# Gate convolution with its rows packed as source, row and channel, in four 32-column tiles

## The chip, the cores and the metric

The kernel runs on one core of one Trainium2 chip. The metric is the device time of one execution in microseconds; three runs of the kernel before gave a median of 13,861.98 us (13,850.41 to 13,873.61). Engines are named as in the profile: PE is TensorE (PEld its weight loads), DVE VectorE, ACT ScalarE, POOL GpSimd, and SPq the queue of SyncE, which here issues nearly all DMAs.

## The reference

A batch of 32 images with 8 channels of 256 x 256 goes through two residual layers, each with a group normalisation ahead of it (4 groups of 2 channels).

```python
# layer 0, on x normalised
grid = drive = x
for _ in range(15):
    mapped = 3.9 * grid * (1.0 - grid)
    local = conv3x3(mapped, K_local, groups=8)         # depthwise
    physics = 0.7 * mapped + 0.3 * local
    grid = 0.85 * physics + 0.15 * drive
cml_out = clip(grid, 0.0001, 0.9999)
h = relu(conv3x3(x, Wp, bp))                           # 8 -> 128
nca_out = sigmoid(conv1x1(h, Wu, bu))                  # 128 -> 8
gin = concatenate([x, cml_out, nca_out], axis=1)       # 24 channels
g = sigmoid(conv1x1(relu(conv3x3(gin, Wg1, bg1)), Wg2, bg2))
layer0 = g * cml_out + (1.0 - g) * nca_out
# layer 1: both operands quantised to +-127, conv3x3 8 -> 8, scaled back, plus bias
```

The gate convolution is the 3 x 3 convolution with Wg1 over the 24 channels of gin, to 8 channels.

## The kernel before

Images are worked in eight groups of four (GB = 4). Five kinds of work, each written as a generator that yields a weight after each piece:

- `prep`/`normalise` (L301): loads x, normalises it, and writes to DRAM scratch a permuted copy for the lattice (xq_s, made by ACT at L370: the pixels of a row ordered by their column modulo four) and a padded high/low pair for NCA (xp_s).
- `lattice` (L396): the 15 steps on grid, a channel of the group's four images at a time, all of it resident in SBUF. A step is three tiles of 6 matmuls (L511), with DVE operations from PSUM (L519, L524), a small POOL product at the edges (L528), and at the end of tiles 1 and 2 an exchange of halo rows by two DMAs each (L474, L475) that the next step needs. After each tile up to three DMAs of a backlog (unit loads d_a, result stores to cm_s; L464) are issued by `background`.
- `nca` (L581): the 8 to 128 convolution (L591, two row tiles of 48 rows), relu on ACT (h, L601), the 128 to 8 product in four 32-column tiles (L608), sigmoid (L626), store to nc_s.
- `gate` (L745): described below.
- the second layer, in a section of its own from L936, after all groups.

TensorE's order is written out by hand: `together` (L870) runs a lattice step and then as many pieces of the filler as keep both in proportion, and `both` (L884) mixes NCA, the gate of the group before, and prep by the totals T_NCA = 520, T_GATE = 340, T_PREP = 34 and T_LATTICE = 709 (L916). The other engines' order is made by the scheduler of the framework from the program's order and its own estimates[...]. The last group's gates run alone at the end (L930).

The gate before: an image is 19 tiles of 14 output rows, with 16 rows x 8 channels on the 128 partitions (two halo rows). A piece p takes two tiles, and there are ten per image, the last with one tile. `stage` (L691) loads nc_s (nb), cm_s (cq) and the raw x (xb, one DMA per tile). `arrange` (L719), called two yields later, unpermutes cq to natural order on POOL (L723), normalises xb on DVE (L729), and makes d = cml - nca and f = x + nca on POOL (L735, L736). The convolution (L795) is three sources x three column shifts x two 64-column halves, with 128 x 128 banded weights gw, spread over three yields of 3.5 and 2.6. Then relu on ACT (L812), and one piece later `finish` (L752): the 1 x 1 product (L758), sigmoid (L760), y = gate * d + f on DVE (L762, L763), statistics (L771 to L773). The store of y to y_s is issued one piece later still (L802).

## Time and profile before

| | |
|---|---|
| median of three runs | 13,861.98 us |
| the profiled execution: its time and span | 13,862.1 us |
| PE busy | 13,134.4 us, 95% |
| DVE, ACT, POOL busy | 59%, 29%, 18% |
| L511 lattice matmuls, on the m_a and the m_b side (these two run at once) | 5,842.6 and 5,809.7 us |
| L591 NCA convolution, high and low weights (overlapping) | 2,685.1 and 2,569.9 us |
| L608 NCA product | 1,155.1 us |
| L795 gate convolution, by source cmb, xnb, nb | 861.4, 847.8 and 847.2 us |
| L758 gate product | 319.8 us |
| DMA moved, share of the 16 engines | 1,496.77 MB, 46% |
| mean granted TensorE clock | 0.975 |

An fp32 matmul appears in the trace as two passes, so a count in the profile is twice the number in the program. A group's busy time counts a stretch once when several of its instructions overlap in it, and matmuls overlap with their neighbours, so prices of matmuls are better read from the start of one to the start of the next. DMA issues do not count as busy time of SP; they are read from SP's queue in the timeline.

### The profile page before, as it was taken

To read this page: it belongs to the slowest core of one execution; us is meant where nothing else is said; L and a number is where in the kernel's file an instruction comes from. 1 tells how busy PE (TensorE), PEld (TensorE's weight loads), DVE (VectorE), ACT (ScalarE), POOL (GpSimd) and SP (SyncE) were. 2 spreads that over 40 slices of the span, in tenths; PEclk is the share of its full clock that TensorE was granted. 3 is DMA by queue.
4 is the path that set the end of the run, shared out by engine and by line. 5 is a ranking of instruction groups with operands and counts; after the bars stand their busy time and mean duration, and the time that the engine had idled before them with its cause. 6 is when DMAs were issued, how large, how long until landed. Compare 5 with 4: busy or idle time off the path is not lost.

```text
span 13862.1 us, 229831 instructions
## 1 busy us (share of the span) xinstructions
PE 13134.4 (95%) x81840; PEld 6403.4 (46%) x81840; DVE 8176.8 (59%) x16402; ACT 4028.2 (29%) x6274; POOL 2454.7 (18%) x4278
## 2 busy tenths in 40 slices
PE   4899999999999999999999999999999999999964
PEld 2445544444444444444444444444444444444322
DVE  5555565566655565555655565555655555555577
ACT  2233223232322223322323223222223222222123
POOL 1001111121111211111111111112111111111310
PEclk8999999999999999999999999999999999999986
DMA  6444444444444444444444444444444433333368
GB/s 152 96 97 99 96 104 112 101 98 101 111 99 103 109 93 108 108 104 93 107 106 101 102 104 103 102 106 108 94 108 110 100 91 84 89 79 89 90 202 257
DMA packets 2287210, 1496.77 MB, mean 108 GB/s; under 512 B 1096576, under 2 KB 2257152, under 8 KB 2285952
## 3 DMA queue, kind: packets, MB, share of 16 engines
q1 hardware_dynamic: 2191360, 1392.13, 43.1%
q10 hardware_dynamic: 94720, 89.93, 2.1%
q8 instruction: 665, 10.90, 0.3%
q14 instruction: 465, 3.81, 0.1%
HBM read 866.48 MB, written 478.69 MB: 97 GB/s over the span
## 4 chain that ended last, share of the span: by engine, by line
PE 81%; DMA 8%; SPq 4%; DVE 3%; issue 1%; ACTq 1%; ACT 0%; POOL 0%; POOLq 0%; DVEq 0%
PE pt L511 36%; PE ph L591 20%; PE pa L795 16%; PE acc L608 7%; DMA yb<-y_s 2%; PE pg L758 2%; DMA im<-xp_s 1%; DVE gt L519 1%; ACTq L1021 1%; DMA m_a<-m_a 1%; DMA xb<-in_x_dram 1%; DMA xp_s<-lo 1%; SPq L464 1%; SPq L569 1%; DVE m_a L524 1%
## 5 line engine op out<-in xcount | busy, mean ns | idle before, releaser
L511 PE MATMUL pt<-m_a,lw 128*64 128x390 f32 x17280 | 5842.6, 496 | 162.0 <-DMA m_a<-m_a 103.3
L511 PE MATMUL pt<-m_b,lw 128*64 128x384 f32 x17280 | 5809.7, 491 | 18.9 <-DVE m_b L430 18.1
L601 ACT ACTIVATE h<-ph,bp_sb 128x512 f32<-128x512 f32 x4096 | 2581.8, 684 | 4845.8 <-PE ph L591 4772.4
L511 PEld LDWEIGHTS pt<-m_a,lw 128*64 128x64 f32 x17280 | 2302.2, 138 | 1795.4 <-issue 1597.2
L511 PEld LDWEIGHTS pt<-m_b,lw 128*64 128x64 f32 x17280 | 2310.1, 138 | 1638.4 <-issue 1522.3
L591 PE MATMUL ph<-im,wp_hi 48*128 48x512 f32 x12288 | 2685.1, 415 | 119.0 <-DMA im<-xp_s 59.4
L519 DVE SCALAR_TENSOR_TENSOR gt<-pt,d_b 128x390 f32<-128x390 f32 x2880 | 1609.3, 559 | 1820.8 <-PE pt L511 1818.2
L519 DVE SCALAR_TENSOR_TENSOR gt<-pt,d_a 128x384 f32<-128x384 f32 x2880 | 1584.1, 550 | 1837.4 <-PE pt L511 1836.7
L591 PE MATMUL ph<-im,wp_lo 48*128 48x512 f32 x12288 | 2569.9, 398 | 0.0
L528 POOL TENSOR_TENSOR m_b<-m_b,junk 128x12 f32<-128x12 f32 x2688 | 817.1, 304 | 8414.1 <-DVE m_b L524 7988.0
L591 PEld LDWEIGHTS ph<-im,wp_hi 48*128 48x128 f32 x12288 | 1312.0, 187 | 969.7 <-DVE m_a L524 180.7
L524 DVE SCALAR_TENSOR_TENSOR m_b<-gt 128x390 f32<-128x390 f32 x2688 | 1557.1, 579 | 46.4 <-DVE gt L519 0.9
L524 DVE SCALAR_TENSOR_TENSOR m_a<-gt 128x384 f32<-128x384 f32 x2688 | 1540.3, 573 | 18.0
L591 PEld LDWEIGHTS ph<-im,wp_lo 48*128 48x128 f32 x12288 | 1309.2, 188 | 218.6
L608 PE MATMUL acc<-h,wu_z 128*32 128x512 f32 x8320 | 1155.1, 598 | 6.1 <-ACT nca L626 5.5
L795 PE MATMUL pa<-cmb,gw 128*64 128x512 f32 (+1 forms) x3840 | 861.4, 580 | 15.5 <-POOL cmb L723 15.5
L795 PE MATMUL pa<-xnb,gw 128*64 128x512 f32 (+1 forms) x3840 | 847.8, 574 | 11.1 <-ACT r L812 11.1
L795 PE MATMUL pa<-nb,gw 128*64 128x512 f32 (+1 forms) x3840 | 847.2, 573 | 0.0
L762 DVE TENSOR_TENSOR gate<-gate,d 128x512 f32<-128x512 f32 x320 | 218.3, 682 | 823.0 <-ACT gate L760 805.0
L812 ACT ACTIVATE r<-pa,bv 128x512 f32<-128x512 f32 x320 | 213.1, 666 | 1650.4 <-PE pa L795 1650.4
L729 DVE TENSOR_SCALAR xnb<-xb,sc 128x256 f32<-128x256 f32 x608 | 305.0, 517 | 596.9 <-DMA xb<-in_x_dram 590.7
L760 ACT ACTIVATE gate<-pg,bv 128x512 f32<-128x512 f32 x320 | 213.2, 666 | 1519.1 <-PE pg L758 1508.1
(133 smaller groups left out, 7225.3 us busy)
## 6 DMA issues: line engine op xcount, KB each, us to landing
im<-xp_s SPq DMA_DIRECT2D x1152, 193.5 KB
im<-xp_s SPq DMA_DIRECT2D x1216, 96.8 KB
d_a<-xq_s SPq DMA_DIRECT2D x2048, 36.0 KB
nb<-nc_s SPq DMA_DIRECT2D x288, 256.0 KB
cq<-cm_s SPq DMA_DIRECT2D x288, 256.0 KB
xb<-in_x_dram SPq DMA_DIRECT2D x544, 128.0 KB
yb<-y_s ACTq DMA_DIRECT2D x28, 2432.0 KB
xp_s<-hi SPq DMA_DIRECT2D x256, 258.0 KB
```

Source lines behind the costliest of these rows:

```text
L511: T.matmul(pt[half], lw[:, c, k, half], beside if part == 2 else own, start=part < 2, stop=part > 0,)
L519: V.scalar_tensor_tensor(gt, pt, FLOOR, d[:, ts, :], ALU.max, ALU.add)
L524: V.scalar_tensor_tensor(to, gt, 1.0, gt, ALU.subtract, ALU.mult)
L528: G.tensor_tensor(edge, edge, junk.unsqueeze(1).to_broadcast([P, 6, 2]), ALU.mult)
L591: T.matmul(ph[:, :n].rearrange("p (h w) -> p h w", w=W), w[64 * i : 64 * i + 48, dx, :], rhs[:, :, dx : dx + W], start=(dx == 0 and w is w ...
L601: S.activation(h[:, :n], ph[:, :n], AF.Relu, bias=bp_sb)
L608: T.matmul(acc[32 * g : 32 * g + 32, :cols], wu_z[:, 24 - 8 * i : 56 - 8 * i], h, start=first, stop=last,)
L729: V.tensor_scalar(xnb[:, k, 1 : 1 + W], xb[:, k, :], sc[:, i : i + 1], sc[:, 1:2], ALU.subtract, ALU.mult,)
L758: T.matmul(pg[half, :cols], gw2[:, half], r1[:, :cols], start=True, stop=True)
L760: S.activation(gt[:, :cols], pg[:, :cols], AF.Sigmoid, bias=bv[:, 1:2])
L762: V.tensor_tensor(three(y), three(gt), d[:, :n, :], ALU.mult)
L795: T.matmul(three[half], gw[:, s * 3 + dx, half], t[:, :n, dx : dx + W], start=(i == 0), stop=(i == 8),)
```

## The change

The rows of the array hold 3 sources x 5 rows x 8 channels = 120 input rows, which give 3 output rows x 8 channels = 24 of 32 columns. Four such tiles stand side by side in the array's columns. A piece t makes 4 tiles x 2 sub-blocks x 3 rows = 24 output rows, so there are 11 per image. All three sources now lie in one scratch tensor gs_s per image, in the lattice's column order (column modulo four first); x is taken in its normalised form and the raw value restored by ACT (f = x * std + mean). The shift by one column, in that order, becomes two slices for each side (PARTS).

```diff
-    xq_s = [dp.tile([C, H, 4, NJ], F32, name=f"xq_s{i}") for i in range(NBUF)]
-    cm_s = [dp.tile([PROWS, C, W], F32, name=f"cm_s{i}") for i in range(NBUF)]
-    nc_s = [dp.tile([PROWS, C, W], F32, name=f"nc_s{i}") for i in range(NBUF)]
+    gs_s = [dp.tile([3, PROWS, C, W], F32, name=f"gs_s{i}") for i in range(NBUF)]
...
-        hp, xp, sp2, gp, bp2 = pool("hp", 12), pool("xp", 4), pool("sp2", 1), pool("gp", 3), pool("bp2", 2)
+        hp, xp, sp2, gp, gip = pool("hp", 12), pool("xp", 4), pool("sp2", 1), pool("gp", 3), pool("gip", 2)
...
-                    o = wk.tile([P, 2, W], F32, name="nca", tag="nca", bufs=3)
+                    o = wk.tile([P, 2, W], F32, name="nca", tag="nca", bufs=2)
                     S.activation(
-                        o, acc.rearrange("p (k w) -> p k w", w=W), AF.Sigmoid, bias=bv[:, 2:3]
+                        o.rearrange("p k (q j) -> p k q j", q=4),
+                        acc.rearrange("p (k j q) -> p k q j", k=2, q=4),
+                        AF.Sigmoid, bias=bv[:, 2:3],
                     )
...
+        def stage(b, t):
+            gin = gip.tile([P, 8, W], F32, name="gin", tag="gin")
+            for j in range(3):
                 nc.sync.dma_start(
+                    gin[40 * j : 40 * j + 40],
+                    dram_ap(gs_s[b % NBUF], j * PART + 24 * t * C * W, [[W, 40], [3 * C * W, 8], [1, W]]),
+                )
+            mix = mixes[(NG8 * b + t) % 2]
+            for i in range(8):
+                nc.sync.dma_start(
+                    mix[32 * (i // 2) : 32 * (i // 2) + 24, :, i % 2, :],
                     dram_ap(
+                        gs_s[b % NBUF], (24 * t + 3 * i + 1) * C * W, [[W, 24], [PART, 3], [1, W]]
                     ),
                 )
+            return gin, mix
+
+        natural = lambda t: t.rearrange("p k (j q) -> p k q j", q=4)
+        phased = lambda t: t.rearrange("p k (q j) -> p k q j", q=4)
+
+        def arrange(sc, gin, mix):
+            d = wk1.tile([P, 2, W], F32, name="d", tag="d")
+            f = wk1.tile([P, 2, W], F32, name="f", tag="f")
+            G.tensor_tensor(natural(d), phased(mix[:, 1]), phased(mix[:, 2]), ALU.subtract)
+            S.activation(
+                natural(f), phased(mix[:, 0]), AF.Identity, bias=sc[:, 0:1], scale=sc[:, 2:3]
+            )
+            G.tensor_tensor(natural(f), natural(f), phased(mix[:, 2]), ALU.add)
+            return gin, d, f
...
+        PARTS = (
+            (1, slice(0, 256), slice(0, 256)),
+            (0, slice(64, 256), slice(0, 192)),
+            (0, slice(1, 64), slice(192, 255)),
+            (2, slice(0, 192), slice(64, 256)),
+            (2, slice(192, 255), slice(1, 64)),
+        )
...
+            for t in range(NG8):
+                gin, d, f = ahead
+                if last:
+                    put(done)
+                    done = finish(*last)
                 pa = ps_a.tile([P, 512], F32, name="pa", tag="acc")
+                three = pa.rearrange("p (k w) -> p k w", w=W)
+                for n, (dx, to, of) in enumerate(PARTS):
+                    for i in range(4):
+                        T.matmul(
+                            three[32 * i : 32 * i + 32, :, to], gw[:120, dx, :],
+                            gin[:120, 2 * i : 2 * i + 2, of],
+                            start=(n == 0), stop=(n == len(PARTS) - 1),
+                        )
+                r1 = wk.tile([P, 512], F32, name="r1", tag="r1")
+                S.activation(r1, pa, AF.Relu, bias=bv[:, 0:1])
+                last = (t, r1, d, f)
+                if t < NG8 - 1:
+                    ahead = arrange(sc, *stage(b, t + 1))
+                elif (b + 1) % GB:
+                    sc, one = begin_gate(b + 1)
+                    staged[b + 1] = sc, arrange(sc, *one)
+                if sums:
+                    sums.pop(0)()
+                yield 3.5
...
-        T_NCA, T_GATE, T_PREP, T_LATTICE = 520.0, 340.0, 34.0, 8 * 45 * 1.97
+        T_NCA, T_GATE, T_PREP, T_LATTICE = 520.0, 158.0, 34.0, 8 * 45 * 1.97
```

Beyond this: the 1 x 1 product in `finish` runs in four 32-column tiles; the sigmoid there writes through `natural`, which turns the result back to natural column order; y is stored by four DMAs per piece instead of one (`put`), each of 24 partitions and two sub-blocks; the y and nca buffers go from three to two; the weights gw come ready from the host as 120 x 3 x 32 instead of being built from the raw weights on DVE; the lattice's loads and stores address gs_s with rows of all channels in between (the runs stay 256 bytes); the statistics take three masks in place of two, and sums over three parts.

## The prediction

> **What bounds the kernel now.** I read the span, the busy shares and the chain first.

> ```profile
> span 13862.1 us, 229831 instructions
> PE 13134.4 (95%) x81840; PEld 6403.4 (46%) x81840; DVE 8176.8 (59%) x16402; ACT 4028.2 (29%) x6274; POOL 2454.7 (18%) x4278
> ...
> PE 81%; DMA 8%; SPq 4%; DVE 3%; issue 1%; ACTq 1%; ACT 0%; POOL 0%; POOLq 0%; DVEq 0%
> ```

> TensorE sets the time: 95% busy, 81% of the chain. The windows view says it more sharply for the middle, where lattice, NCA and gate run interleaved: of 8,200 us TensorE is busy 8,094. And its own waits there are tiny. First the windows view, then the waits view of TensorE, both between 3,400 and 11,600 us:

> ```profile
> 3400.00:11600.00 8200.00, 8094.35 (x51126) 3943.34 (x51122) 4875.13 (x10093) 2407.02 (x3766) 1545.29 (x2668) 0.99 0.45 103
> ```

> (columns: PE, PEld, DVE, ACT and POOL busy with instructions, clock, DMA share, GB/s)

> ```profile
> PE ph L591 <- DVE gt L519: 31.9, 32, 2.2
> PE pt L511 <- DMA m_a<-m_a: 24.7, 32, 2.9
> ```

> The second wait is the one to keep in mind: a lattice step needs the rows that SP's exchange DMAs (L474, L475) bring from the step before. It costs nothing now, because gate and NCA matmuls lie between two steps. The TensorE timeline shows such a stretch and the prices of the gate:

> ```profile
> 6002.31 2.80 PE L795 MATMUL pa<-xnb,gw 128*64 128x512 f32 x12
> 6004.94 1.03 PE L758 MATMUL pg<-r,gw 128*64 128x512 f32 x4
> 6005.79 0.49 PE L511 MATMUL pt<-m_a,lw 128*64 128x390 f32 x1
> ...
> 6014.85 1.92 PE L608 MATMUL acc<-h,wu_z 128*32 128x512 f32 x16
> 6016.71 2.80 PE L795 MATMUL pa<-cmb,gw 128*64 128x512 f32 x12
> 6019.33 0.49 PE L511 MATMUL pt<-m_a,lw 128*64 128x390 f32 x1
> ```

> From start to start, one source's 12 half-width instructions take 2.63 us and the second gate matmul 0.85 us; 16 instructions of L608 (two sets of four 32-column tiles, each in two passes) take 1.86 us, 0.93 a set. Last, SP's queue around the next gate piece:

> ```profile
> 6040.28 0.56 SPq L475 DMA_DIRECT2D m_a<-m_a  x1
> 6040.94 0.38 SPq L669 DMA_DIRECT2D nc_s<-nca  x1
> 6041.42 0.40 SPq L677 DMA_DIRECT2D nc_s<-nca  x1
> 6041.87 1.38 SPq L569 DMA_DIRECT2D im<-xp_s  x3
> 6043.29 0.42 SPq L802 DMA_DIRECT2D y_s<-gate  x1
> 6043.76 0.46 SPq L695 DMA_DIRECT2D nb<-nc_s  x1
> 6044.26 0.50 SPq L700 DMA_DIRECT2D cq<-cm_s  x1
> 6044.80 1.29 SPq L709 DMA_DIRECT2D xb<-in_x_dram  x2
> ```

> Every DMA holds SP for 0.4 to 0.65 us, one after the other, and the exchanges stand in this same queue. Adding all issue durations of SP in the trace from 3,400 to 11,600 us gives 4,954 us for 9,493 DMAs, and the gap between two is 0.044 us: SP is some 66% taken.

> [...] L608's four tiles start 6 ns apart and share 0.43 us per pass. [...]

> **The change part by part.** The execution profiled is 13,862.1 us, next to the median of 13,861.98, so I work from the span. The lattice runs from 86 to 12,930 us, the first gate's loads start at 1,445, the last group's four images run alone to 13,295, and the quantised second layer takes the other 567. Of the 32 gates 28 lie beside the lattice.

> *Gate matmuls on TensorE.* Before, a full piece p costs 3 x 2.63 + 0.85 = 8.74 us; nine of these and the half one (about 4.4, from 1.30 us per source in the tail's timeline) are 83.0 us per image. After, one piece t streams 256+192+63+192+63 column pairs, 512+384+126+384+126 = 1,532 columns, through four tiles at once. At L608's 0.93 us per 512 that is 2.8 us. The two parts of 126 columns may not hide their weight loads (a pass is 0.106 us there, a load 110 ns at L608): between 0 and 0.44 us, I take 0.2. With the second matmul 0.93, a piece is 3.95 us (3.5 to 4.3), eleven are 43.5. Saving 39.5 us x 28 = 1,106. Fewer changes between kinds of matmul (30 pieces per image become 11, about 0.1 us each, as from 6016.6 to 6016.71) give 55 more: **-1,160 us** beside the lattice.

> *The tail.* Four gates alone take 357 us now, TensorE-bound. After, TensorE needs 4 us per piece but SP issues 15 DMAs: with the tail's shorter issues (0.32 to 0.4 us) 6.2 us[...]. 44 x 7 + 14 = 322: **-35 us**. If loads and pieces don't overlap, it is +40.

> *Start.* The nine weight builds of gw go (27 small DVE operations and more): **-5 us**.

> *VectorE, GpSimd, ScalarE.* DVE loses L729 (305 us in all), and has 352 pieces for 304 full ones, +160. POOL loses 608 copies of 701 ns and keeps two adds per piece. ACT gets f, 352 x 1.06 (half of L370, which also reads in steps of four: 2,114 ns for 1,024), and up to 0.4 more for the permuted gate and nca: +630 us, 29% becomes 35%. All of it lies under TensorE: priced at nothing while the queues flow.

> *DMA.* A gate piece moves 1.57 MB instead of about 1.0, 320 MB in all; the engines' share goes from 0.45 to some 0.6. Not a bound.

> *SP's queue.* Per image: out go 10 nb (0.458), 10 cq (0.455), 19 xb (0.615) and 10 stores (0.38), 25 us; in come 121 loads (0.45, as nb) and 44 stores (0.38), 71 us, in bursts of 15 DMAs, 7.3 us with the gaps. Per group of four images SP goes from about 1,090 us out of 1,641 to about 1,290 out of 1,475. That is 88%.

> *What is late next: the exchange.* From the trace, 3,000 to 12,000 us: the fill between two steps is 7.6 us at the median; the last exchange is issued 3.6 us after the step's last matmul (a quarter over 5.1) and its packets are through 1.4 us after the issue begins, so landed about 1.6. The second tile needs it at the fill plus 1.97 us. Median margin: 7.6 + 1.97 - 3.6 - 1.6 = 4.4, or 3.7 taken step by step; a quarter below 1.8. After, the planner's weights leave (520+158+34)/120 = 5.9 of fill per step instead of 7.45, in fewer and coarser pieces: following its rule through a group, 22 of 120 gaps hold 3.5 or less. SP after a gate burst is late: in that slot 2.5 (DVE ready) + 1.2 (exchange) + 7.3 + 1.3 (NCA) + 1.8 (background) = 14.1 us, against the next exchange being ready at 6.5 (fill) + 5.9 + 0.2 = 12.6 and often at 9.6: 1.5 to 4.5 us late. The following gap is about 5.2, and needs 0.3 + late + 1.2 + 1.6: a stall of 0 to 3 us, say 1.7 for each of 44 bursts, plus 0.8 for the 22 thin gaps: 75 + 18 us, about 90 per group. Seven groups: **+630 us** (bounds 100, if bursts fall where SP has time, and 1,250, if each burst costs 4 us). Below nothing is excluded: no DMA is taken off SP.

> Sum: 13,862 - 1,160 - 35 - 5 + 630 = 13,292, say **13,300**.

> **The rivals.** *The cover holds* (chance 0.22): two or three steps share one burst, SP catches up between, and only 100 to 300 us are lost. 12,660 + 100 to 300, about 12,850. For it: SP waits 2,012 us for DVE at L474 in the same stretch, all of it slack. Against it: the burst is concentrated, and the slack lies in other steps.

> *The new loads block ACT and POOL* (slower, 0.15): d, f and the sum are put right behind the loads (`arrange(sc, *stage(...))`), where before a piece's loads had two pieces' time. The eight mix DMAs end a burst of 15, so they land about 7 + 7 + 1.6 us after the step, some 15.5, while NCA's activations (h, L601) and the lattice's edge products (L528) queue behind them in ACT and POOL. In front of NCA work of the same gap that is up to 7 us of TensorE standing for PSUM buffers. For it: POOL already waits 803.7 us for cq. Against: these waits harm nothing today, and operations whose inputs are late are seen placed behind others. It decides from (1,200 - 630) / 308 = 1.9 us per piece on top; at 4 us, with the exchange's loss, the time is 13,300 + 1,230 = 14,530.

> *The tiles don't run at once* (0.01 within the last): a piece would cost four times 3.73, about 15 us, slower; L608 speaks against it.

> **How the numbers follow.** Likeliest case 0.52 (12,950 to 13,650); cover holds 0.22; partly blocked but still faster 0.08 (13,650 to 13,834); unchanged within 0.2%, about what can be measured here, 0.03; slower 0.15. Faster 0.82. The range from 12,650 to 13,950 leaves out 0.05 below and 0.13 above.

> **What would show it.** Right: pa near 2.8 to 3.2 us per piece with four tiles of the same start; about 165 SP issues per image of 0.38 to 0.5 us; TensorE's waits at pt for m_a up from 103 us to several hundred; TensorE's busy time near 11,950. Wrong: short parts of 0.5 us or more each (weight loads bind); waits of ph or pt for ACT h or POOL m_b in the hundreds (the second rival); hardly any new idle time (the first).

## The result

| | before | after |
|---|---|---|
| median of four runs | 13,860.1 us | 14,790.0 us |
| ratio, 95% interval | | 1.067 (1.065 to 1.068) |
| span of the profiled execution | 13,862.1 us | 14,789.1 us |

The change makes the kernel 6.7% slower; the prediction was 13,300 us, 4% faster. The page of the changed kernel, the lines that answer to those of before:

```profile
span 14789.1 us, 243934 instructions
...
PE 12548.6 (85%) x86064; PEld 6392.5 (43%) x86064; DVE 8036.6 (54%) x15812; ACT 4699.0 (32%) x6690; POOL 2159.0 (15%) x3656
...
PE 44%; DMA 30%; SPq 17%; DVE 4%; issue 3%; ACTq 1%; ACT 1%; POOL 0%; POOLq 0%; DVEq 0%
```

TensorE does less, as intended, but DMAs and SP's queue now hold 47% of the chain that was TensorE's at 81%. The windows view of the same 8,200 us as before the change (3,400 to 11,600 us), and TensorE's waits in it (us in total, times, longest):

```profile
3400.00:11600.00 8200.00, 7221.39 (x50272) 3700.42 (x50268) 4461.05 (x9122) 2652.33 (x3772) 1271.26 (x2137) 0.93 0.54 120
```

```profile
PE pt L508 <- DMA m_a<-m_a: 753.9, 184, 13.8
PE ph L588 <- DMA im<-xp_s: 89.9, 63, 7.2
```

TensorE is idle for 980 of the 8,200 us (106 before), its clock is 0.93 instead of 0.99, and the wait for the lattice's exchange has gone from 25 to 754 us. The gate itself is cheap, as TensorE's timeline shows:

```profile
6002.55 1.06 PE L753 MATMUL pg<-r,gw 128*32 128x512 f32 x8
6003.43 2.76 PE L803 MATMUL pa<-gin,gw 120*32 120x512 f32 x40
6006.13 0.50 PE L588 MATMUL ph<-im,wp_hi 48*128 48x512 f32 x2
```

From start to start the product takes 0.88 us and the convolution 2.70, so a piece takes 3.58. Where the time went, I read from all TensorE records and the stretches of granted clock, which is either 1.0 or 0.5 in these traces. "Work" is busy time, in which the part that fell into a stretch at clock 0.5 counts half (the lattice's matmuls follow each other 0.67 us apart there and 0.33 otherwise, as shown below); "half clock" is the other half of that part, the price of the lower clock; "idle" is the rest of the span.

| us | before | after | difference |
|---|---|---|---|
| work | 12,935 | 11,708 | -1,227 |
| half clock | 199 | 841 | +642 |
| idle | 728 | 2,240 | +1,512 |
| span | 13,862 | 14,789 | +927 |

The idle time, by the matmul that ends it: lattice on m_a 162 to 1,230 us; the gate's convolution on its loads 27 to 325, of which 234 in the tail (the last group's gates, which run alone at the end); NCA on im 119 to 240. SP's queue ahead of one such stall:

```profile
6007.84 2.00 SPq L461 DMA_DIRECT2D gs_s<-d_b  x3
6010.26 1.55 SPq L785 DMA_DIRECT2D y_s<-gate  x4
6011.85 1.28 SPq L700 DMA_DIRECT2D gin<-gs_s  x3
6013.24 7.99 SPq L706 DMA_DIRECT2D mix<-gs_s  x8
6021.49 0.72 SPq L461 DMA_DIRECT2D gs_s<-d_b  x1
6022.26 0.90 SPq L461 DMA_DIRECT2D gs_s<-d_a  x2
6023.27 0.63 SPq L471 DMA_DIRECT2D m_a<-m_a  x1
```

A burst, the loads and stores of one gate piece, is four stores, three gin loads and eight mix loads. Here they take 11 us, and the exchange of the step comes after them. The eight mix loads need 7.99 us where eight issues of 0.37 need 3: single records show the first five issued 0.4 us apart and the last three at 6016.2, 6018.3 and 6020.9. SP's waits over the whole run name what they stand for:

```profile
SPq L706 <- DMA gin<-gs_s: 1625.0, 942, 3.9
SPq L471 <- DVE m_a L521: 1510.8, 637, 9.4
```

942 times is close to three for each of 352 pieces. In the trace the DMAs issued by SP (19,454) and ACT (236) carry the same eight semaphores in turn: 19,113 of 19,682 have that of the DMA eight places earlier (the expectations below call this the ring). The 6th to 8th mix load stand for the three gin loads, whose semaphores they carry: in the 301 bursts whose loads follow each other directly, 891 of 903 such issues stood, and each began 16 to 17 ns after the last update of that semaphore. TensorE at the other end:

```profile
6021.28 0.39 PE L588 MATMUL ph<-im,wp_lo 48*128 48x512 f32 x2
6026.74 0.88 PE L508 MATMUL pt<-m_a,lw 128*64 128x390 f32 x1 [5.06 <-DMA m_a<-m_a]
6026.86 0.87 PE L508 MATMUL pt<-m_b,lw 128*64 128x384 f32 x1
6027.41 0.86 PE L508 MATMUL pt<-m_a,lw 128*64 128x390 f32 x1
```

TensorE is idle for 5 us, and then its matmuls follow each other 0.67 us apart on a side, not 0.33: the granted clock is 0.5 from 6024.08 to 6030.91. For every exchange I took the end of DVE's write of m_a ("ready"), the start and end of its issue, and the end of its eighth packet ("landed"), from 3,400 to 11,600 us; "after a burst" are those next in line behind a piece's loads, and "late" is the time from ready to the start of the issue. Before, the first exchange of a step is 0.3 to 0.4 us late, behind a burst or not. After, it is 6.3 us late behind a burst (203 of 530 steps) and 0.8 us otherwise. The loads of a burst begin 4.5 us (median) ahead of the time when the next exchange is ready, and last 10.6 us (mean).

### The profile page after: what moved, and what is told of

Its sections match the earlier page's. It is cut to its first block, busy times and chain, and to the rows that moved or that the text cites. A ratio compares the mean times of both kernels' runs of the same rounds, so it can differ in the third digit from the quotient of the medians.

```text
span 14789.1 us, 243934 instructions
## 1 busy us (share of the span) xinstructions
PE 12548.6 (85%) x86064; PEld 6392.5 (43%) x86064; DVE 8036.6 (54%) x15812; ACT 4699.0 (32%) x6690; POOL 2159.0 (15%) x3656
## 4 chain that ended last, share of the span: by engine, by line
PE 44%; DMA 30%; SPq 17%; DVE 4%; issue 3%; ACTq 1%; ACT 1%; POOL 0%; POOLq 0%; DVEq 0%
PE pt L508 24%; PE ph L588 12%; DMA mix<-gs_s 11%; DMA gin<-gs_s 5%; SPq L461 4%; DMA im<-xp_s 4%; PE acc L605 4%; DMA m_a<-m_a 3%; PE pa L803 2%; SPq L471 2%; DMA yb<-y_s 2%; SPq L566 2%; SPq L785 2%; SPq L472 2%; SPq L700 2%
## 5 line engine op out<-in xcount | busy, mean ns | idle before, releaser
L508 PE MATMUL pt<-m_a,lw 128*64 128x390 f32 x17280 | 6011.0, 524 | 1229.8 <-DMA m_a<-m_a 1130.1
L508 PE MATMUL pt<-m_b,lw 128*64 128x384 f32 x17280 | 5943.5, 516 | 19.2 <-DVE m_b L427 18.4
L588 PE MATMUL ph<-im,wp_hi 48*128 48x512 f32 x12288 | 2750.8, 420 | 240.4 <-DMA im<-xp_s 200.9
L588 PE MATMUL ph<-im,wp_lo 48*128 48x512 f32 x12288 | 2638.5, 405 | 0.0
L803 PE MATMUL pa<-gin,gw 120*32 120x126 f32 (+2 forms) x14080 | 1102.8, 461 | 325.4 <-DMA mix<-gs_s 186.3
L803 PEld LDWEIGHTS pa<-gin,gw 120*32 120x32 f32 x14080 | 483.1, 118 | 1111.3 <-issue 1028.5
L755 ACT ACTIVATE gate<-pg,bv 128x512 f32<-128x512 f32 x352 | 435.1, 1236 | 1409.7 <-PE pg L753 1355.3
L722 POOL TENSOR_TENSOR d<-mix 128x512 f32<-128x512 f32 x352 | 456.4, 1297 | 2028.1 <-DMA m_a<-m_a 506.8
L723 ACT ACTIVATE f<-mix,sc 128x512 f32<-128x512 f32 x352 | 466.6, 1326 | 767.2 <-DMA m_a<-m_a 281.9
L758 DVE TENSOR_TENSOR gate<-gate,d 128x512 f32<-128x512 f32 x352 | 253.3, 719 | 685.5 <-ACT gate L755 585.6
L726 POOL TENSOR_TENSOR f<-f,mix 128x512 f32<-128x512 f32 x352 | 542.7, 1542 | 345.0 <-ACT f L723 338.6
```

Source lines behind the costliest of these rows:

```text
L508: T.matmul(pt[half], lw[:, c, k, half], beside if part == 2 else own, start=part < 2, stop=part > 0,)
L588: T.matmul(ph[:, :n].rearrange("p (h w) -> p h w", w=W), w[64 * i : 64 * i + 48, dx, :], rhs[:, :, dx : dx + W], start=(dx == 0 and w is w ...
L722: G.tensor_tensor(natural(d), phased(mix[:, 1]), phased(mix[:, 2]), ALU.subtract)
L723: S.activation(natural(f), phased(mix[:, 0]), AF.Identity, bias=sc[:, 0:1], scale=sc[:, 2:3])
L726: G.tensor_tensor(natural(f), natural(f), phased(mix[:, 2]), ALU.add)
L803: T.matmul(three[32 * i : 32 * i + 32, :, to], gw[:120, dx, :], gin[:120, 2 * i : 2 * i + 2, of], start=(n == 0), stop=(n == len(PARTS) - 1),)
```

## The experiments

Times are medians of four runs; beside them the ratio to the kernel before with its interval. The kernel before ran at 13,893 to 13,905 us in these series, some 40 us above its time in the first; differences from 14,790 are uncertain by about as much. All edits are to the changed kernel unless another is named.

**1. gin from ACT's queue.**

```diff
-                nc.sync.dma_start(
+                nc.scalar.dma_start(
                     gin[40 * j : 40 * j + 40],
```

> The changed kernel with the three gin loads of a piece issued from ACT's queue; mix loads and all else stay on SP. Four theories of the lost time. A: SP has eight semaphores for its DMAs, so the sixth mix issue waits until the first gin load, eight DMAs back, has landed; SP stands about 5 us per piece, the exchanges behind it are late, TensorE idles and then runs at half clock. B: the 15 issues of a piece alone fill SP. C: ACT and POOL stand on mix with f and d. D: the 1.5 MB per piece crowd the DMA engines. A: SP's wait at mix goes from 1,625 us to under 200, TensorE's wait for m_a from 1,130 to under 350, time 13,300 +- 250. B: three of 15 issues leave SP, 14,500. C and D: same data at the same time, 14,800 or a little more.

14,863 us, 1.070 (1.068 to 1.071). No gain: SP stands for gin all the same, now at other lines (595 + 284 + 278 + 245 + 153 us at five of them, 1,556 in all):

```profile
SPq L471 <- DVE m_a L521: 1640.6, 683, 11.4
SPq L461 <- DMA gin<-gs_s: 595.1, 163, 9.0
SPq L785 <- DMA gin<-gs_s: 284.0, 118, 6.3
```

SP waits for loads that it did not issue, 1,556 us here: the eight semaphores are shared by both queues. So theory A was not tested here.

**2. mix ahead of gin.** The loop of the eight mix loads is put before that of the three gin loads.

> The changed kernel with the eight mix loads issued ahead of the three gin loads. A: the burst itself passes, and the wait for gin moves to the eighth DMA behind each gin load; the exchanges often stand in front of that: half of the loss is back, 14,000 to 14,500. B and D: 14,790. C: mix lands some 5 us earlier, so most of the loss is back, 13,400.

14,610 us, 1.051 (1.049 to 1.052), 180 less, outside what any of the theories said. The wait for gin moves from mix to the background's DMAs (411 us at L461) and NCA's row loads (265 at L566), which now stand eight places later; in all it is 958 us in place of 1,625.

**3. Small gin loads.**

```diff
-                    gin[40 * j : 40 * j + 40],
-                    dram_ap(..., [[W, 40], [3 * C * W, 8], [1, W]]),
+                    gin[40 * j : 40 * j + 40, 0:1],
+                    dram_ap(..., [[W, 40], [3 * C * W, 1], [1, W]]),
```

> The changed kernel, but the gin loads bring only the first of the eight sub-blocks (40 KB instead of 320 KB each) into buffers cleared at the start, so the gate convolution runs on incomplete input; the number of DMAs and of all other instructions stays. A and D: the loads land before the eighth DMA behind them is due, 13,250 +- 250, SP's wait at mix under 200 us. B: 14,750. C: mix lands earlier, 13,400.

13,388 us, 0.963 (0.962 to 0.965), as A and D had it. The count of DMAs is as in the changed kernel, and 1,400 us are gone. SP no longer waits for gin, half clock falls from 841 to 455 us, the idle time on m_a from 1,230 to 510, the tail from 536 to 309. The gate also need not wait for the seven sub-blocks left out (its idle time falls from 325 to 89 us).

**4. arrange one piece later.** `ahead = stage(b, t + 1)`, and `arrange(sc, *ahead)` at the start of the piece that follows.

> The changed kernel with d, f and the sum made one piece later, at the start of the piece that uses the loaded gin, when mix has long landed. C: most of the loss is back, 13,300. A, B and D: 14,790 +- 100.

14,861 us, 1.070 (1.068 to 1.071). More time for d and f buys nothing, so theory C, the rival in which ACT and POOL are blocked, is refuted.

**5. gin from POOL's queue** (`nc.gpsimd.dma_start` for gin).

> The changed kernel with the three gin loads of a piece issued from POOL's queue. The run with them on ACT showed that SP and ACT draw on the same eight semaphores, so SP stood behind gin as before, 1,556 us in all, and A was not tested. POOL's DMAs should have semaphores of their own. A (SP stands on the semaphore ring): SP's waits for gin are gone, 13,400 to 13,700, with something lost to POOL's edge products behind the issues. D (the 960 KB of gin crowd the DMA engines): same bytes at the same time, 14,700 to 14,900.

14,241 us, 1.026 (1.024 to 1.027): 550 less, between the two theories. The bytes go on costing: with small gin loads the time was 13,388 us. But 550 us is more than the 1,056 issues of 0.4 us (some 420 us) that SP lost; its 1,625 us of waits for gin went too (none of its nine longest waits, down to 83 us, is for gin), so here another issuer saved more than issue time.

**6. Small gin, one mix load of eight** (`range(1)` in experiment 3).

> The kernel with the small gin loads, and in addition only the first of the eight mix loads; gate convolution and blend run on incomplete data. 8 DMAs per piece instead of 15, little data. It shows what the 15 issues alone cost: with small gin and all mix loads the time was 13,388 against 12,660, worked out from the matmuls alone. B, as priced in the prediction (+630 us from a burst that is 7.3 us long): the burst is 3.7 us, most of the 630 us goes, 12,850 +- 150. If the thin gaps between lattice steps are what costs: 13,300.

12,917 us, 0.930 (0.928 to 0.931), 470 less than experiment 3 and as forecast. A burst is eight short DMAs; the exchange behind it is 1.0 us late, and TensorE's wait for m_a falls to 235 us. With most loads gone, the time is near the rival "the cover holds" (12,850): the thinner filler alone costs little.

**7. Loads spread over three yields.** A piece yields 0.9, 1.6 and 1.2; ahead of each one gin load and two or three mix loads.

> The changed kernel with a gate piece in three yields (finish; three parts of the convolution; the rest) and in each one gin load with two or three mix loads, instead of all 11 after the last. Same DMAs, same matmuls, same totals. A: no more than one gin load is among eight DMAs in flight, so SP hardly stands; and the bursts are 5 DMAs: 13,200 +- 250, faster than both kernels. D: the data is the same and only spread, 14,000 to 14,400.

14,427 us, 1.038 (1.037 to 1.040), 363 less: near D, 1,230 above what A had. Exchanges after the first load of a piece are 3.0 us late in place of 6.3, but the others 1.3 in place of 0.8, and SP still waits 1,094 us for gin.

**8. Packed layout.**

```diff
-    gs_s = [dp.tile([3, PROWS, C, W], ...)]
+    gs_s = [dp.tile([PROWS, C, 3, W], ...)]
...
+            nc.sync.dma_start(gin[:120], dram_ap(gs_s[b % NBUF], 24 * t * 3 * C * W,
+                [[W, 120], [9 * C * W, 8], [1, W]]))
+            for i in range(4):
+                nc.sync.dma_start(mix[32 * i : 32 * i + 24]..., dram_ap(gs_s[b % NBUF],
+                    (24 * t + 6 * i + 1) * 3 * C * W, [[3 * W, 24], [9 * C * W, 2], [1, 3 * W]]))
```

> The scratch tensor of an image is laid out as row, channel, source instead of source, row, channel. The same bytes then come in by one gin load of 120 partitions (rows, channels and sources are one run of lines) and four mix loads with 3 KB packets, in place of three and eight; the rows of gw follow the new order. A piece issues 9 DMAs with its four stores, not 15, and one of them is large. All work of the engines stays as in the changed kernel. My theory (the burst of issues and the landing of three large loads in SP's ring delay the exchange, and the idle halves TensorE's clock): near the variant with a small gin and one mix load (12,917 us), plus what remains for the bytes: 13,150 us, between 12,950 and 13,450, faster than both kernels; TensorE busy in half clock 600 to 900 us, wait of the lattice for m_a's DMA below 450 us. Rival (the loads' bytes crowd the DMA engines however few DMAs carry them): nearly all of the 1,400 us between the changed kernel and the small gin stays, so 14,200 us or more, with a mean packet as long as in the changed kernel.

14,331 us, 1.031 (1.030 to 1.033), 1,180 above my theory. Six issues fewer, with larger packets for mix (2.48 million packets in all, where there were 2.64), gave 460 us. The bytes are the same, and the ring is not gone either: SP still waits 954 us for gin, 598 of it with the exchange itself, which now stands eight places behind gin:

```profile
SPq L471 <- DMA gin<-gs_s: 383.9, 96, 5.6
SPq L472 <- DMA gin<-gs_s: 214.2, 72, 5.3
```

**9. The same with gin from POOL:**

> As the packed layout, and the one gin load is issued from POOL's queue instead of SP's, so it holds no place in the ring of semaphores that SP and ACT share, and SP has one issue less in a piece. My theory: with one large load in a burst of five the ring hardly stops SP any more, so that little is left to gain: within 100 us of the packed layout from SP (in the changed kernel the same move gave 550 us). Rival (the ring still holds SP for each large load): 200 us or more faster than the packed layout from SP.

14,180 us, 1.020 (1.018 to 1.022), 150 less, between the two. SP's waits for gin are gone (954 to under 1 us), so in this layout their end, with one issue less, is worth no more than 150 us. The single gin load of 960 KB also slows what runs beside it: in the packed kernel the exchange behind a burst is issued 3.5 us late and then needs 2.8 us (mean of the first of its DMAs) from the end of its issue to landing; the others need 1.0.

**10. The exchange from POOL's queue, full loads.**

```diff
-                nc.sync.dma_start(t[0::16, below, :], t[14::16, above, :])
-                nc.sync.dma_start(t[15::16, above, :], t[1::16, below, :])
+                nc.gpsimd.dma_start(t[0::16, below, :], t[14::16, above, :])
+                nc.gpsimd.dma_start(t[15::16, above, :], t[1::16, below, :])
...
-            return gin, mix
+            return gin, still        # a constant tile
```

> The changed kernel with the lattice's halo exchange issued from POOL's queue instead of SP's. So that POOL never stands behind a mix load, d and f are made from a constant tile instead of mix (mix is still loaded); the gate's d and f are therefore left out of the result, with POOL's and ACT's work on them unchanged. In the changed kernel the exchange that follows a gate burst starts 6.3 us after its data is ready, on average, the others 0.8 to 1.4 us. My theory (the burst ahead of the exchange in SP's queue is what costs): the exchange that follows a burst is no later than the others, whatever the burst and its bytes do, and the time falls to 13,000 to 13,500 us with half-clock busy time below 900 us. Rival (the bytes fill the DMA engines, or TensorE lacks filler work to cover any exchange): above 14,200 us, the wait for m_a's DMA above 800 us as before.

14,133 us, 1.017 (1.015 to 1.018). Half of each theory. The exchange is now issued 0.6 us after it is ready, burst or not, as mine had it; but the four DMAs next after the first gin load of a piece need 2.7 to 3.6 us from the end of their issue to land, those of other steps 1.4 to 2.1. The queueing has become crowding. TensorE's waits for the exchange are shorter and more; in the changed kernel they were 1,130 us in 310 times, the longest 14.9:

```profile
PE pt L510 <- DMA m_a<-m_a: 836.7, 397, 8.2
```

**11. Packed layout, burst right after the exchange.** The lattice pops the pending load after the exchange of tile 2; arrange stands at the start of its piece.

```diff
                                 elif not a2b:
                                     exchange(m_a[s], k)
+                        if i == 2 and wanted:
+                            wanted.pop(0)[1]()
```

> The packed layout (one gin load, four mix loads), and the loads of a piece are not issued where the gate's piece ends, but by the lattice directly after the exchange of a step, so that the burst has the longest time before the next exchange (arrange moves to the start of its piece, which alone changed nothing). In the packed kernel a burst starts 4.5 us (median) ahead of the time at which the next exchange is ready, and that exchange is 3.5 to 4.3 us late, the others 0.8 to 1.3 us. My theory: a burst of some 6 us then fits ahead of the next exchange; lateness after bursts falls to 1.5 us or less, and the time to 13,200 to 13,700 us, faster than the kernel before. Rival (the place of the burst is nothing, its bytes are what costs, or the scheduler keeps it where it was): within 150 us of the packed kernel's 14,331 us.

14,830 us, 1.068 (1.066 to 1.070): 500 us slower than the packed kernel; neither theory had that. SP's queue and TensorE's waits of this kernel:

```profile
6045.47 0.57 SPq L472 DMA_DIRECT2D m_a<-m_a  x1
6046.07 0.46 SPq L701 DMA_DIRECT2D gin<-gs_s  x1
6046.64 3.01 SPq L706 DMA_DIRECT2D mix<-gs_s  x4
6049.69 1.32 SPq L461 DMA_DIRECT2D gs_s<-d_a  x3
6055.05 1.83 SPq L568 DMA_DIRECT2D im<-xp_s  x4
```

```profile
PE ph L590 <- DMA im<-xp_s: 793.7, 260, 27.0
PE pt L508 <- DMA m_a<-m_a: 552.5, 196, 13.5
```

The burst goes where it was sent and takes 3.6 us. But the eighth DMA after gin is NCA's row load im, and it stands from 6051.0 to 6055.05, until gin has landed, 9 us after its issue. In the packed kernel TensorE waited 995 us for m_a and 169 for im; here 553 and 794. One wait was exchanged for another.

**12. The same place in the changed kernel:**

> The changed kernel with the loads of a piece issued by the lattice directly after the exchange of a step; nothing else is changed but arrange's place. Its burst takes some 10 us, about as long as the time that there is before the next exchange is ready. My theory: lateness after bursts falls from 6.3 to 2 to 4 us, and the time to 13,900 to 14,400 us, not below the kernel before. Rival (the place is nothing): within 150 us of 14,790 us.

15,455 us, 1.112 (1.110 to 1.113), worse than the changed kernel in the same way, by 665 us; both theories missed it.

**13. Experiment 11 with gin from POOL:**

> The packed layout with its burst directly after the exchange, as in the aligned packed kernel (14,830 us), and the gin load issued from POOL. In that kernel the gin load lands some 9 us after its issue, and the DMA eight places later, a row load of NCA, waits for it in SP's ring for 4 us. Theory (the ring undid the alignment): without it SP's burst is 3 us long, the exchange after a burst is less than 2 us late, and the time falls below the 14,180 us of the packed kernel with gin from POOL, to 13,600 to 14,000 us. Rival (the place right after the exchange is bad in itself, since it puts gin's packets beside the exchange's own or moves other loads back): 14,180 us or above.

14,217 us, 1.022 (1.020 to 1.024): 613 us back, where the same move gave 150 in the packed kernel, and the exchange after a burst is 1.6 us late in place of 4.8. So the shared semaphores undid the alignment. But it is no better than experiment 9 with the burst where it was, as the rival had it: the place of the burst gains nothing.

**14. Packed layout, exchange from POOL,** with d and f from mix.

> The packed layout (one gin load of 120 partitions, four mix loads), the exchange issued from POOL's queue, arrange one piece later; all results made as in the changed kernel. Taken alone, the packed layout gave 460 us and the exchange from POOL 657 us of the changed kernel's 14,790. If the two costs (the queue, and the many loads) add, 13,670 us, faster than before (13,900). If they are mostly one cost, about 14,050 us. If d on POOL, which waits for mix, now holds the exchange behind it, 14,300 us or more. I take 13,850 us, between 13,600 and 14,150.

14,428 us, 1.038 (1.036 to 1.040), 580 above what I took, and slower than the packed kernel with the exchange on SP.

```profile
PE pt L508 <- DMA m_a<-m_a: 1243.2, 441, 11.5
```

The exchange is issued 0.6 us after it is ready, and after the start of a burst it lands 3.6 to 4.2 us after the end of its issue. As I read it, on SP it stood behind part of gin's transfer, and from POOL it runs beside all of it. POOL's waits for mix come to 215 us, so I hold the crowding for the cause, not d; no run here separates the two.

**15. Experiment 10 with small gin loads.**

> The exchange from POOL's queue with d and f from a constant tile, as in the earlier run (14,133 us), and the gin loads bring in only the first of eight sub-blocks, 40 KB each, into cleared tiles: gate rows beyond it, d and f are left out of the result. If queueing behind the burst and gin's bytes are one cost, this is no faster than the small gin with the exchange on SP (13,388 us) by more than 150 us. If they are two costs that add, 14,133 - 1,400 = 12,730 us. My theory has both parts: a ring that holds SP for gin's landing is gone in either, so 13,000 us, between 12,900 and 13,250, with the exchange landed 3 us after it is ready, after a burst or not.

12,987 us, 0.935 (0.933 to 0.936), as forecast. With small loads the exchange lands 1.3 to 1.6 us after the end of its issue, where it needed 2.7 to 3.6 with full ones: the crowding is gin's bytes. With experiments 3 and 10 it makes a table:

| us | exchange on SP | exchange on POOL |
|---|---|---|
| full gin loads | 14,790 | 14,133 |
| one sub-block of eight | 13,388 | 12,987 |

Taking the exchange out of SP's queue gains 401 to 657 us (it also takes the exchange's own issues from SP, and in these two runs d and f do not stand for mix), small gin loads 1,146 to 1,402. Both together gain 1,803, 256 less than the sum of the two. So most of the loss is gin's bytes, and only some 256 us of that act through the exchange's place in SP's queue.

**16. No mix; d and f made by TensorE from gin.** From the packed kernel: selection weights pick cml - nca and x * std + nca out of the gin tile; gin has three buffers and is loaded two pieces ahead.

```diff
+                for pt, w in ((pd, gw[:120, 3, :]), (pf, fw[:120])):
+                    for i in range(4):
+                        T.matmul(pt[32 * i : 32 * i + 32], w, gin[:120, 2 * i : 2 * i + 2, :]...,
+                                 start=True, stop=True)
...
+                V.tensor_tensor(yl, yl, pd, ALU.mult)
+                for k in range(2):          # natural(y) = (pf + mean) + yl
+                    V.scalar_tensor_tensor(natural(y[:, k]), phased(pf[k]), sc[:, 0:1],
+                                           phased(yl[k]), ALU.add, ALU.add)
```

> The packed layout without mix: d = cml - nca and f = x * std + nca are made by TensorE from the gin tile with selection weights (two more products of four 32-column tiles, 0.9 us each by the gate product), the mean is added by DVE, and gin has three buffers and is loaded two pieces ahead. POOL and ACT have no arrange work; a piece issues 5 DMAs, not 9, and 144 x 4 KB less. All results are made. TensorE gets 352 x 1.8 = 620 us of work. My theory (what the loads cost beyond the change's saving is their issues, their bytes and the tail's loads): against the packed kernel's 14,331 us, m_a's idle time falls by some 500 us, the tail's by 170, im's by 100, the half clock by 250 to 300, less the 620 that come in: 13,850 us, between 13,600 and 14,150. Rival (the gin bytes alone cause nearly all): 14,600 us or more.

13,615 us, 0.979 (0.978 to 0.981): faster than both kernels, 2% below the kernel before and at the low end of what I took.

```profile
PE 12581.7 (92%) x91696; PEld 6255.6 (46%) x91696; DVE 8066.1 (59%) x16196; ACT 4092.0 (30%) x6338; POOL 1147.3 (8%) x2950
```

```profile
PE pt L506 <- DMA m_a<-m_a: 405.0, 189, 8.4
...
PE ph L586 <- DMA im<-xp_s: 118.7, 53, 27.2
```

Against the packed kernel: work +546, half clock -354, idle -910, together -718. TensorE does more, and its idle time falls by more than that: a piece has four issues and 576 KB less, the exchange after a burst is 0.7 us late, and the work lies as cover between steps. The run changes several things at once (loads, bytes, work, buffers), so it does not tell their shares.

**17. The same with gin from POOL:**

> The same with gin issued from POOL's queue, which has no arrange work now. The move gave 150 us in the packed kernel and 550 in the changed one. My theory: 13,700 us, between 13,450 and 14,000, so perhaps just faster than the kernel before (13,900). Rival: as for the same kernel with gin on SP, no gain from the move.

13,601 us, 0.978 (0.976 to 0.980). The intervals overlap: no gain from the move any more.

## Why the prediction was wrong

*The step that failed is the exchange's term,* "Seven groups: **+630 us** (bounds 100 ... and 1,250)", as the price of all lateness. Its mechanism was right: behind a gate burst the exchange is late, and TensorE waits for m_a. It was sized too low, and it priced the lattice's waits alone. Against the prediction's own sum:

| us | predicted | measured |
|---|---|---|
| TensorE's work (gate, tail and start) | -1,200 | -1,227 |
| idle time before the lattice's matmuls on m_a | +630 | +1,068 |
| idle time elsewhere, most of it gate and NCA standing for loads | 0 | +444 |
| half clock | 0 | +642 |
| together | -570 | +927 |

The exchange's own idle time came out inside its bound of 1,250; the two terms at nothing carried the sum out of the predicted range. Three things were missing.

- "SP after a gate burst is late: in that slot ... 7.3": the issues were priced rightly (0.37 to 0.40 us each), but the 11 loads alone last 10.6 us, since the last of them stand for gin's landing. The exchange is 6.3 us late where I had 1.5 to 4.5. SP waited for earlier DMAs before too, for 215 of the 8,200 us, and I had put all gaps down to issue; after the change it is 1,232.
- "the engines' share goes from 0.45 to some 0.6. **Not a bound.**" The share went to 0.54 only. But it is a mean, and the exchange needs the engines in the very microseconds in which gin's packets run. With the exchange out of SP's queue, full gin loads still cost 1,146 us against small ones (experiments 10 and 15), and the exchange landed 1.4 to 2.0 us later beside them. Not all of the 1,146 is crowding, since small loads also end SP's 1,808 us of waits for gin there; but the 514 us of it that are idle time on m_a no longer pass through SP's queue. This step was wrong outright.
- The clock is in no step. In the traces half-clock stretches (83 before, 347 after) begin on one grid of 3.413 us, to within 1.2 ns, and all but one of each last a multiple of it, to within 1%. A window of this grid need not be wholly idle for half clock to follow. Of the changed kernel's windows at full clock, those with TensorE idle for under 30% were never followed by half clock (0 of 3,080; before, 4 of 3,720), those with 30 to 60% in 62 of 183 cases, those with more in 285 of 309. Gaps shorter than a window count too: half clock followed within 0.5 us after 96% of the gaps of over 4 us, 51% of those of 2 to 3 us, and 30% of those of 1 to 2 us. Gaps over 3.4 us went from 54 to 259, and a half-clock stretch cost 2.4 us on average (841 us in 347).

*The gate matmuls* (-1,160). A piece took 3.58 us, not 3.95: the short parts hide their weight loads (a load takes 0.110 us; a part of 126 columns takes 0.108 us a pass, one of 512 takes 0.433), and the convolution is 2.70. That the work came out near -1,200 is partly luck. It counts all 32 images, for which the prediction's own prices give some -1,330. Counted from the start of each matmul to the next, the gate's two products fell by 1,414 us, but the lattice's matmuls, unchanged in number, took 194 us more. Why they did is open.

*The tail* (-35): it grew from 361 to 536 us, +175. A piece takes 12.2 us there and not 7 (my estimate, of which the trace showed 6.2 us of issues), because gin lands late and loads are only one piece ahead. Small gin loads (experiment 3) bring it to 309, three buffers without mix (experiment 16) to 301.

*DVE, ACT and POOL at nothing:* right, as far as experiment 4 shows; and TensorE's waits for ACT and POOL stay small (28 us for ACT, none for POOL, of the 980). The permuted gate write costs ACT 1.24 us, where the plain one took 0.67, and is hidden.

*SP's queue:* issues as priced; SP's issue time from 3,400 to 11,600 us rose from 4,954 to 5,296 us. What was not priced is the standing for earlier DMAs.

*The rivals.* "The cover holds" is what the kernel would do without its loads (experiment 6). "The new loads block ACT and POOL" gave a time near to the measured one (14,530), for a reason that experiment 4 refutes.

The 1,146 us of gin's bytes are, between experiments 10 and 15: idle time on m_a 514, tail and im about 190, half clock 369; some 80 us of it stay open. So does why the lattice's matmuls take longer.

## What to carry to other kernels

Where a small transfer feeds every step, price a burst of loads three times: as issues in the queue (0.37 to 0.40 us each here), as landing times that later issues stand for (1,625 us here), and as packets beside the small transfer (the exchange landed 1.4 to 2.0 us later here); the mean DMA share, 0.54, told nothing of the last two. An idle gap of TensorE costs more than itself when the work after it runs at half clock; here half clock followed 96% of the gaps over 4 us and 51% of those of 2 to 3 us, and a stretch of it cost 2.4 us on average. If data is in SBUF already, picking it out on TensorE can beat loading it a second time: some 1.8 us of matmuls per piece replaced four loads in experiment 16 and, together with a third buffer, gave 5% against the packed kernel.
